# Four graph-attention layers on one core: broadcasting a row of factors by DMA and a ScalarE copy instead of TensorE transposes

## The chip, the cores and the metric

The kernel runs on one core of one Trainium2 chip. The metric is the time of one execution on the device in microseconds (us). TensorE (PE) multiplies matrices, VectorE (DVE), ScalarE (ACT) and GpSimd (POOL) work element by element, and SyncE (SP) here only issues DMA transfers. Each engine has its own queue of instructions, and semaphores make one engine wait for another.

## The reference, cut to what matters

The input x has 16 batch items of 1024 nodes with 256 features, in float32. Four layers follow each other, and each adds to x the output of a graph attention over one 1024 x 1024 adjacency matrix. Layers 0 and 2 have 4 heads of 64 features, layers 1 and 3 have one head of 256.

```python
h = jnp.maximum(_layernorm(x, axis=-1), 0.0)
# one layer, one head, with Wh = h @ W:
e = e_src[:, None] + e_dst[None, :]          # e_src = Wh @ a[:D], e_dst = Wh @ a[D:]
e = jnp.where(e > 0, e, slope * e)
e = jnp.where(adj, e, -inf)
h_prime = softmax(e, axis=-1) @ Wh
x = x + elu(h_prime)                         # relu in layer 3
```

The kernel uses that exp of a leaky relu of a sum is a maximum of two products. A factor that depends on the row i alone falls out of the softmax, so that the weight of node j for node i is mask(j, i) times max(g(i), r(j)), and the rest of the exponent, which depends on j alone, is multiplied into the rows of Wh. With j on the 128 partitions, r(j) is a scalar of the partition, but g(i) has to stand in every partition as a row of 1024 numbers. How this row comes to be in all partitions is what the change is about.

## The kernel before

A **step** is one layer of one batch item; there are 64 steps, 32 of a 4-head layer and 32 of a 1-head layer, and four batch items are interleaved. Every step is cut into eight **positions**, one for each group of its aggregation. Each engine's instructions run in the order of the program. The preparation of step n + 2 is spread over the positions from the start of step n on (in the steady part of the program) by this table, whose entries are positions after the plan was made:

```python
WBUFS = 21
PREPARATION = (0, 0, 1, 2, 3, 3, 4, 4, 5, 5, 5, 5, 6, 6, 7, 7, 8)
# pieces: stats(0), stats(1), normalise(0), normalise(1), transpose x2, project x4,
#         transpose x2, project x4, factors
```

So `factors` of a step falls on position 0 of the step ahead of it. The pieces that matter here:

```python
def normalise(half):                                    # ScalarE
    xn = st["xn", half] = prep.tile([P, HALF, F], F32, name="t4", bufs=3)
    for q in range(HALF):
        c = half * HALF + q
        nc.scalar.activation(xn[:, q, :], xs[b][:, c, :], AF.Identity,
                             bias=st["shift"][:, c:c + 1], scale=st["rstd"][:, c:c + 1])

def transpose(half, k):                                 # TensorE, then ScalarE to hT
    pt = ps_p.tile([P, HALF, P], F32, name="pp")        # ps_p has two buffers
    for q in range(HALF):
        nc.tensor.transpose(pt[:, q, :], st["xn", half][:, q, k * P:(k + 1) * P], ident)
    nc.scalar.activation(st["hT", half][:, k, :], pt.rearrange("p q i -> p (q i)"), AF.Relu)

def project(c):                                         # TensorE from hT; ScalarE empties pw
    pw = ps_p.tile([P, F + 2 * H], F32, name="pp")
    ...

def factors():
    ...                                                 # rcol, gcol: exp on ScalarE
    nc.gpsimd.tensor_scalar(gcol, gcol, EXP_SHIFT, None, op0=ALU.min)

def broadcast(n, h):                                    # g(i) into all partitions
    g = state[n]["g", h] = ps_g.tile([P, N], F32, name="g")
    for c in range(C):
        nc.tensor.transpose(g[:, c * P:(c + 1) * P],
                            state[n]["gcol"][:, c, h:h + 1].to_broadcast([P, P]), ident)

def weights(n, h, jc):                                  # VectorE, 128 x 1024
    w = state[n]["w", h, jc] = work.tile([P, N], F32, name="w", bufs=WBUFS)
    nc.vector.scalar_tensor_tensor(w, state[n]["g", h], state[n]["rcol"][:, jc, h:h + 1],
                                   mask[:, jc, :], op0=ALU.max, op1=ALU.mult)
```

`aggregate` multiplies eight such tiles `w` of a head with `whx` on TensorE into `acc` (two buffers) and copies `acc` to `y` on ScalarE. What ends a step, `finish`, is spread over positions 0 to 3 of the next step:

```python
def scaled(half):                                       # GpSimd: yh *= r; then
    e = st["e", half] = prep.tile([P, HALF * H, D], F32, name="t4", bufs=3)
    nc.gpsimd.tensor_scalar(e, yh, 0.0, -3.0e38, op0=ALU.min, op1=ALU.max)
def exponential(half):
    nc.scalar.activation(st["e", half], st["e", half], AF.Exp)
def add(half):                                          # not in the last layer
    nc.vector.scalar_tensor_tensor(e, e, -1.0, yh, op0=ALU.add, op1=ALU.max)
    nc.gpsimd.tensor_add(xh, xh, e)
return [(0, divide), (0, lambda: scaled(0)), (1, lambda: scaled(1)),
        (1, lambda: exponential(0)), (2, lambda: exponential(1)),
        (2, lambda: add(0)), (3, lambda: add(1))]
```

`xn` and `e` are both named `t4` and share one ring of three buffers. One position of the main loop is, in the order of the program:

```python
emit_tiles(place[n, h, C - 1] + 1, must=True)   # tiles w that this group needs
aggregate(n, h, i0, per)
while ending and ending[0][0] <= k:             # pieces of the last step's finish
    ending.pop(0)[1]()
prepare(8 * n + k)                              # pieces of preparation due here
emit_tiles(min(done["tiles"] + ahead, done["free"] + WBUFS))   # tiles w ahead of need
```

`emit_tiles` calls `broadcast` for a head when the next tile is within four of it, and only once the preparation of its step is complete.

Of the kernel before, what the change touches and what calls it, by code (L numbers as in the profile page):

```python
# [24 lines left out]
F32 = mybir.dt.float32  # L25
# [3 lines left out]
AF = mybir.ActivationFunctionType  # L29
# [4 lines left out]
P = 128  # L34
# [1 line left out]
SHIFT = 60.0  # L36
EXP_SHIFT = math.exp(SHIFT)
STREAMS = 4
WBUFS = 21
PREPARATION = (0, 0, 1, 2, 3, 3, 4, 4, 5, 5, 5, 5, 6, 6, 7, 7, 8)  # L40


LAYERS = [
# [8 lines left out]
def kernel(ctx: ExitStack, tc: tile.TileContext, x, adj, ws, avs, out):  # L52
    nc = tc.nc
    B, N, F = x.shape
    C = N // P
# [5 lines left out]
    ident = const.tile([P, P], F32, name="ident")  # L61
# [17 lines left out]
    with tc.tile_pool(name="wprep", bufs=2) as wp, tc.tile_pool(  # L79
        name="wpsum", bufs=2, space=PSUM  # L80
    ) as wps:
        for l, (H, slope, hs, _) in enumerate(LAYERS):
# [3 lines left out]
            for part in range(2):  # L86
                nc.scalar.dma_start(
                    out=a_bc[:, part],
                    in_=bass.AP(tensor=avs[l].tensor, offset=avs[l].offset + part * D,
                                ap=[[0, P], [hs, H], [1, D]]),  # L90
# [24 lines left out]
    with tc.tile_pool(name="mprep", bufs=2) as mp, tc.tile_pool(  # L115
        name="mpsum", bufs=2, space=PSUM
# [16 lines left out]
    small = ctx.enter_context(tc.tile_pool(name="small", bufs=4))  # L133
    work = ctx.enter_context(tc.tile_pool(name="work", bufs=2))
    ps_g = ctx.enter_context(tc.tile_pool(name="ps_g", bufs=2, space=PSUM))
    ps_acc = ctx.enter_context(tc.tile_pool(name="ps_acc", bufs=2, space=PSUM))
    ps_p = ctx.enter_context(tc.tile_pool(name="ps_p", bufs=2, space=PSUM))

    L = len(LAYERS)
# [2 lines left out]
    state = [dict() for _ in steps]  # L142
# [5 lines left out]
    def preparation(n):  # L148

        b, l = steps[n]  # L150
        H, slope, _, _ = LAYERS[l]
        D = F // H
        st = state[n]

        def stats(half):
            if half == 0:
                st["mv"] = small.tile([P, C, 2], F32, name="mv")
                st["bn"] = small.tile([P, C, 6], F32, name="bn")
            for c in range(half * HALF, (half + 1) * HALF):
                nc.vector.bn_stats(st["bn"][:, c, :], xs[b][:, c, :])  # L160
                nc.vector.bn_aggr(st["mv"][:, c, :], st["bn"][:, c, :])  # L161
            if half == 1:
                rstd = st["rstd"] = small.tile([P, C], F32, name="rstd")
                nc.gpsimd.tensor_scalar(rstd, st["mv"][:, :, 1], EPS, None, op0=ALU.add)
                nc.gpsimd.tensor_tensor(rstd, rstd, neghalf, op=ALU.pow)  # L165
                shift = st["shift"] = small.tile([P, C], F32, name="shift")
                nc.gpsimd.tensor_tensor(shift, st["mv"][:, :, 0], rstd, op=ALU.mult)
                nc.gpsimd.tensor_scalar(shift, shift, -1.0, None, op0=ALU.mult)

        def normalise(half):  # L170
# [6 lines that stand above are left out]
        def transpose(half, k):  # L177
            if k == 0:
                st["hT", half] = prep.tile([P, K, HALF * P], F32, name="hT")
            pt = ps_p.tile([P, HALF, P], F32, name="pp")  # L180
            for q in range(HALF):
                nc.tensor.transpose(pt[:, q, :], st["xn", half][:, q, k * P:(k + 1) * P], ident)  # L182
            nc.scalar.activation(st["hT", half][:, k, :], pt.rearrange("p q i -> p (q i)"),  # L183
                                 AF.Relu)

        def project(c):
            if c == 0:
                st["whx"] = prep.tile([P, C, H, D + 1], F32, name="whx", bufs=3)
                st["sd"] = small.tile([P, C, 2 * H], F32, name="sd")
            whx = st["whx"]  # L190
            half, q = divmod(c, HALF)
            pw = ps_p.tile([P, F + 2 * H], F32, name="pp")
            for k in range(K):
                nc.tensor.matmul(pw, lhsT=st["hT", half][:, k, q * P:(q + 1) * P],  # L194
                                 rhs=wx[l][:, k, :], start=(k == 0), stop=(k == K - 1))
            nc.scalar.activation(whx[:, c, :, D], pw[:, F + H:F + 2 * H], AF.Exp, bias=nbias[l],  # L196
                                 scale=slope)
            nc.scalar.activation(st["sd"][:, c, :], pw[:, F:F + 2 * H], AF.Copy)
            if H == 1:
                nc.scalar.activation(whx[:, c, 0, 0:D], pw[:, 0:D], AF.Copy,  # L200
                                     scale=whx[:, c, 0, D:D + 1])
            else:
                nc.scalar.activation(whx[:, c, :, 0:D],  # L203
                                     pw[:, 0:F].rearrange("p (h d) -> p h d", h=H), AF.Copy)
                nc.gpsimd.tensor_tensor(whx[:, c, :, 0:D], whx[:, c, :, 0:D],  # L205
                                        whx[:, c, :, D:D + 1].to_broadcast([P, H, D]),
                                        op=ALU.mult)

        def factors():
            sd = st["sd"]  # L210
            rcol = st["rcol"] = small.tile([P, C, H], F32, name="rcol")
            nc.scalar.activation(rcol, sd[:, :, H:2 * H], AF.Exp, bias=rbias[l],
                                 scale=1.0 - slope)
            gcol = st["gcol"] = small.tile([P, C, H], F32, name="gcol")
            nc.scalar.activation(gcol, sd[:, :, 0:H], AF.Exp, bias=rbias[l],
                                 scale=-(1.0 - slope))
            nc.gpsimd.tensor_scalar(gcol, gcol, EXP_SHIFT, None, op0=ALU.min)  # L217

        out = [lambda: stats(0), lambda: stats(1), lambda: normalise(0), lambda: normalise(1)]
        for half in range(2):  # L220
            out += [lambda half=half, k=k: transpose(half, k) for k in range(K)]
            out += [lambda c=c: project(c) for c in range(half * HALF, (half + 1) * HALF)]

        return list(zip(PREPARATION, out + [factors], strict=True))

    def broadcast(n, h):

        g = state[n]["g", h] = ps_g.tile([P, N], F32, name="g")
        for c in range(C):
            nc.tensor.transpose(g[:, c * P:(c + 1) * P],  # L230
                                state[n]["gcol"][:, c, h:h + 1].to_broadcast([P, P]), ident)

    def weights(n, h, jc):

        w = state[n]["w", h, jc] = work.tile([P, N], F32, name="w", bufs=WBUFS)
        nc.vector.scalar_tensor_tensor(w, state[n]["g", h], state[n]["rcol"][:, jc, h:h + 1],  # L236
# [72 lines left out]
    def groups(n):  # L309
        if LAYERS[steps[n][1]][0] == 1:  # L310
# [3 lines left out]
    tiles = [(n, h, jc) for n, (b, l) in enumerate(steps) for h in range(LAYERS[l][0])  # L314
             for jc in range(C)]
    place = {t: i for i, t in enumerate(tiles)}
    done = {"tiles": 0, "g": 0, "free": 0, "prepared": 0, "wanted": 0}
    agenda = []

    def prepare(upto):  # L320

        while agenda and (agenda[0][0] <= upto or agenda[0][1] < done["wanted"]):
            _, n, piece, last = agenda.pop(0)
            piece()
            if last:
                done["prepared"] = n + 1

    def plan(n, at):
        new = preparation(n)
        agenda.extend((at + k, n, piece, i == len(new) - 1) for i, (k, piece) in enumerate(new))  # L330
        agenda.sort(key=lambda a: a[:2])

    def emit_tiles(upto, must=False):
        while done["tiles"] < min(upto, len(tiles)):
            i = done["tiles"]

            while done["g"] <= min(i + C // 2, len(tiles) - 1):
                n, h, _ = tiles[done["g"]]
                if n >= done["prepared"]:
                    if i < done["g"] or not must:  # L340
                        break
                    done["wanted"] = n + 1
                    prepare(-1)
                broadcast(n, h)
                done["g"] += C
            if i >= done["g"]:
                return
            weights(*tiles[i])
            done["tiles"] += 1
# [8 lines left out]
    for n in range(2):  # L358
        plan(n, -99)
        prepare(0)  # L360
    ending = []
    with tc.manual_schedule():
        for n in range(len(steps)):
            for k, (h, i0, per) in enumerate(groups(n)):
# [10 lines left out]
                ahead = 4 if per > 1 else 2  # L375
                emit_tiles(min(done["tiles"] + ahead, done["free"] + WBUFS))
            for _, piece in ending:
# [42 lines left out]
```

## Time and profile before

| What | Value |
|---|---|
| Time, median of 3 runs | 2822.34 us (2819.63 to 2822.93) |
| Span of the profiled execution | 2823.2 us |
| DVE busy | 1986.5 us, 70% |
| ACT busy | 1054.9 us, 37% |
| POOL busy | 897.0 us, 32% |
| DMA, mean over the span | 16 GB/s |

Busy time is the sum of an engine's instructions; those of PE are pipelined, so that a busy PE is not PE at its peak. The chain of work that ended last is followed back from the last instruction, at each step to what released it or to the instruction before it on its engine. The list of waits gives for each pair of waiter and releaser the total in us, the number of times and the longest. In the timeline, a line gives the start, the duration, the engine, the line of the kernel, the operation, output and inputs, and in square brackets the idle time just before it and who ended it.

### The profile page before, as it was taken

How to read it: one execution, taken by the hardware profiler on the slowest of the kernel's cores; microseconds unless marked ns; L12 is line 12 of the kernel's file. 1: busy time of each engine (PE TensorE's matmuls, PEld its weight loads, DVE VectorE, ACT ScalarE, POOL GpSimd, SP SyncE). 2: the span in 40 equal slices, each digit the busy share in tenths (PEclk: the TensorE clock that was granted, in tenths of full speed). 3: DMA queues.
4: the chain of work that ended last, by engine and by line, in shares of the span. 5: the costliest groups of instructions: out<-in, count | busy, mean ns of one | idle time of the engine just before them, and what ended most of it. 6: DMA issues, size and time to landing. Idle time of an engine off the chain costs nothing.

```text
span 2823.2 us, 90054 instructions
## 1 busy us (share of the span) xinstructions
PE 2675.6 (95%) x41296; PEld 2387.0 (85%) x41296; DVE 1986.5 (70%) x2569; ACT 1054.9 (37%) x3041; POOL 897.0 (32%) x909
## 2 busy tenths in 40 slices
PE   1899999999999999999999999999999999999998
PEld 1788888888988888888988889888898888888887
DVE  6597675576975678748777469667696577875672
ACT  0423424343333343343344343343333334344331
POOL 0233424233223244243242243333423324324221
PEclk9999999999999999999999999999999999999999
DMA  4000000000000000000100000000010000000000
GB/s 143 7 3 2 2 2 2 2 32 9 25 32 15 18 2 3 2 1 32 32 2 32 31 2 3 2 2 17 16 33 17 16 32 2 3 2 1 17 17 30
DMA packets 38842, 45.60 MB, mean 16 GB/s; under 512 B 3136, under 2 KB 37440, under 8 KB 38464
## 3 DMA queue, kind: packets, MB, share of 16 engines
q1 hardware_dynamic: 35776, 38.80, 4.1%
q8 instruction: 324, 5.31, 0.8%
q10 hardware_dynamic: 2688, 1.05, 0.1%
q14 instruction: 54, 0.44, 0.1%
HBM read 23.07 MB, written 16.78 MB: 14 GB/s over the span
## 4 chain that ended last, share of the span: by engine, by line
PE 89%; DVE 5%; ACT 3%; DMA 1%; POOL 1%; issue 1%; DVEq 0%; ACTq 0%; SPq 0%; POOLq 0%
PE acc L252 64%; PE pp L194 16%; PE g L230 5%; PE pp L182 4%; DVE w L236 3%; ACT whx L196 1%; ACT whx L200 1%; DMA a_bc<-in_L_gnn_a 1%; ACT y L256 1%; DVE bn L160 0%; ACT whx L203 0%; DVE mask L129 0%; POOL gcol L217 0%; DVE t L292 0%; DVE mv L161 0%
## 5 line engine op out<-in xcount | busy, mean ns | idle before, releaser
L252 PE MATMUL acc<-whx,w 128*64 128x65 f32 x36864 | 1939.1, 241 | 21.7 <-DVE w L236 21.6
L252 PEld LDWEIGHTS acc<-whx,w 128*64 128x64 f32 x36864 | 1749.9, 145 | 180.0 <-issue 41.1
L236 DVE SCALAR_TENSOR_TENSOR w<-g,rcol,mask 128x1024 f32<-128x1024 f32 x1280 | 1544.1, 1273 | 419.7 <-PE acc L252 249.5
L256 ACT ACTIVATE y<-acc 128x260 f32<-128x260 f32 (+1 forms) x512 | 197.8, 386 | 1433.0 <-PE acc L252 1433.0
L194 PE MATMUL pp<-wx,hT 128*128 128x258 f32 (+1 forms) x2048 | 509.1, 392 | 2.0 <-ACT hT L183 2.0
L277 POOL TENSOR_TENSOR y<-y,r 128x1024 f32<-128x1024 f32 x128 | 242.8, 1898 | 814.3 <-DVE r L273 814.3
L194 PEld LDWEIGHTS pp<-wx,hT 128*128 128x128 f32 x2048 | 379.4, 190 | 67.1 <-ACT hT L183 3.0
L205 POOL TENSOR_TENSOR whx<-whx 128x256 f32<-128x256 f32 x256 | 157.7, 617 | 599.0 <-ACT whx L203 599.0
L293 POOL TENSOR_TENSOR x<-x,t 128x1024 f32<-128x1024 f32 x96 | 227.2, 2366 | 227.2 <-DVE t L292 227.2
L174 ACT ACTIVATE t<-x,shift,rstd 128x256 f32<-128x256 f32 x512 | 265.2, 590 | 47.7 <-POOL x L293 42.5
L273 DVE RECIPROCAL r<-y 128x32 f32<-128x32 f32 (+1 forms) x64 | 17.7, 277 | 324.5 <-ACT y L256 324.5
L196 ACT ACTIVATE whx<-pp,nbias 128x4 f32<-128x4 f32 (+1 forms) x512 | 135.3, 264 | 192.0 <-PE pp L194 179.1
L230 PE MATMUL g<-ident,gcol 128*128 128x128 f32 x1280 | 169.6, 275 | 38.8 <-POOL gcol L217 38.8
L160 DVE BATCH_NORM_STATS2 bn<-x 128x6 f32<-128x256 f32 x512 | 200.7, 392 | 2.2 <-DMA x<-in_x 2.2
L230 PEld LDWEIGHTS g<-ident,gcol 128*128 128x128 f32 x1280 | 142.1, 137 | 59.4 <-POOL gcol L217 50.9
L182 PE MATMUL pp<-ident,t 128*128 128x128 f32 x1024 | 153.0, 282 | 27.8 <-ACT t L174 12.7
L182 PEld LDWEIGHTS pp<-ident,t 128*128 128x128 f32 x1024 | 110.9, 141 | 70.5 <-ACT whx L200 28.0
L183 ACT ACTIVATE hT<-pp 128x512 f32<-128x512 f32 x256 | 145.9, 595 | 20.7 <-PE pp L182 19.1
L292 DVE SCALAR_TENSOR_TENSOR t<-t,y 128x1024 f32<-128x1024 f32 x96 | 118.6, 1235 | 39.4 <-ACT t L286 39.4
L200 ACT ACTIVATE whx<-pp,whx 128x256 f32<-128x256 f32 x256 | 121.4, 474 | 0.0
L165 POOL TENSOR_TENSOR rstd<-rstd,neghalf 128x8 f32<-128x8 f32 x64 | 106.7, 1666 | 5.3
L161 DVE BATCH_NORM_AGGREGATE mv<-bn 128x2 f32<-128x6 f32 x512 | 92.8, 181 | 16.9
(35 smaller groups left out, 593.7 us busy)
## 6 DMA issues: line engine op xcount, KB each, us to landing
x<-in_x SPq DMA_DIRECT2D x16, 1024.0 KB, 5.3
out<-x SPq DMA_DIRECT2D x32, 512.0 KB, 3.1
a_raw<-in_adj SPq DMA_DIRECT2D x8, 512.0 KB, 3.7
a_bc<-in_L_gnn_a ACTq DMA_DIRECT2D x8, 128.0 KB, 5.9
wx<-in_L_gnn_W SPq DMA_DIRECT2D x4, 256.0 KB, 12.4
```

The costliest lines, as they stand in the source:

```text
L160: nc.vector.bn_stats(st["bn"][:, c, :], xs[b][:, c, :])
L174: nc.scalar.activation(xn[:, q, :], xs[b][:, c, :], AF.Identity, bias=st["shift"][:, c:c + 1], scale=st["rstd"][:, c:c + 1])
L182: nc.tensor.transpose(pt[:, q, :], st["xn", half][:, q, k * P:(k + 1) * P], ident)
L194: nc.tensor.matmul(pw, lhsT=st["hT", half][:, k, q * P:(q + 1) * P], rhs=wx[l][:, k, :], start=(k == 0), stop=(k == K - 1))
L196: nc.scalar.activation(whx[:, c, :, D], pw[:, F + H:F + 2 * H], AF.Exp, bias=nbias[l], scale=slope)
L205: nc.gpsimd.tensor_tensor(whx[:, c, :, 0:D], whx[:, c, :, 0:D], whx[:, c, :, D:D + 1].to_broadcast([P, H, D]), op=ALU.mult)
L230: nc.tensor.transpose(g[:, c * P:(c + 1) * P], state[n]["gcol"][:, c, h:h + 1].to_broadcast([P, P]), ident)
L236: nc.vector.scalar_tensor_tensor(w, state[n]["g", h], state[n]["rcol"][:, jc, h:h + 1], masks[LAYERS[steps[n][1]][3]][:, jc, :], op0=ALU.m ...
L252: nc.tensor.matmul(acc[o % P:o % P + cols, q, :], lhsT=st["w", h, jc][:, o:o + cols], rhs=st["whx"][:, jc, h, :], start=(jc == 0), stop=(j ...
L256: nc.scalar.activation(st["y"][:, i0:i0 + per, h, :], acc, AF.Copy)
L277: nc.gpsimd.tensor_tensor(yh, yh, r[:, :, None].to_broadcast([P, HALF * H, D]), op=ALU.mult)
L293: nc.gpsimd.tensor_add(xh, xh, e)
```

## The change: a row in DRAM, a broadcasting DMA and a copy

The change takes the broadcast off TensorE. A new piece `rows`, one position after `factors`, transposes all of a step's `gcol` at once on TensorE, copies the result to SBUF on ScalarE and stores it as rows of 1024 numbers in DRAM. A DMA then reads one row into all 128 partitions (`fetch`), and ScalarE copies it from there into the PSUM tile `g` that VectorE reads as before. Rows are fetched up to two heads ahead of the head that was broadcast last. Two more buffers of 128 x 1024 for the fetched rows take their room from the tiles `w`, of which 19 are left. The rows of x are normalised by ScalarE in both kernels, in `normalise`, which the change leaves as it is.

```diff
-WBUFS = 21
-PREPARATION = (0, 0, 1, 2, 3, 3, 4, 4, 5, 5, 5, 5, 6, 6, 7, 7, 8)
+WBUFS = 19
+PREPARATION = (0, 0, 1, 2, 3, 3, 4, 4, 5, 5, 5, 5, 6, 6, 7, 7, 8, 9)
...
+    dram = ctx.enter_context(tc.tile_pool(name="dram", bufs=4, space=bass.MemoryType.DRAM))
...
+        def rows():
+            pt = ps_p.tile([C * H, P], F32, name="pp")
+            nc.tensor.transpose(pt, st["gcol"].rearrange("p c h -> p (c h)"), ident)
+            gT = small.tile([C * H, P], F32, name="gT", bufs=2)
+            nc.scalar.activation(gT, pt, AF.Copy)
+            st["grow"] = dram.tile([H, C, P], F32, name="grow")
+            nc.sync.dma_start(out=st["grow"].rearrange("h c i -> c h i"), in_=gT)
...
-        return list(zip(PREPARATION, out + [factors], strict=True))
+        return list(zip(PREPARATION, out + [factors, rows], strict=True))
+
+    def fetch(n, h):
+        gs = state[n]["gs", h] = work.tile([P, N], F32, name="gs", bufs=2)
+        nc.sync.dma_start(out=gs, in_=state[n]["grow"][h].rearrange("c i -> (c i)")
+                          .partition_broadcast(P))
 
     def broadcast(n, h):
         g = state[n]["g", h] = ps_g.tile([P, N], F32, name="g")
-        for c in range(C):
-            nc.tensor.transpose(g[:, c * P:(c + 1) * P],
-                                state[n]["gcol"][:, c, h:h + 1].to_broadcast([P, P]), ident)
+        nc.scalar.activation(g, state[n]["gs", h], AF.Copy)
...
+    def fetch_heads():      # called when a step is prepared, and after each broadcast
+        while done["gs"] < min(done["g"] + 2 * C, len(tiles)):
+            n, h, _ = tiles[done["gs"]]
+            if n >= done["prepared"]:
+                break
+            fetch(n, h)
+            done["gs"] += C
```

More of the change, by code (lines that the diff above doesn't have):

```diff
@@ L316 @@
     place = {t: i for i, t in enumerate(tiles)}
-    done = {"tiles": 0, "g": 0, "free": 0, "prepared": 0, "wanted": 0}
+    done = {"tiles": 0, "g": 0, "gs": 0, "free": 0, "prepared": 0, "wanted": 0}
     agenda = []
@@ L326, in prepare @@
                 done["prepared"] = n + 1
+                fetch_heads()
     def plan(n, at):
@@ L345, in emit_tiles @@
                 done["g"] += C
+                fetch_heads()
             if i >= done["g"]:
```

## The prediction, made before the changed kernel was run

> **What bounds the kernel now.** I read the page first: busy times, then the chain of work that ended last. TensorE is busy nearly all the time, and the chain lies on it for 89%. The transposes that broadcast g (line 230) are 5% of the span there, about 141 us.
>
> ```profile
> PE 2675.6 (95%) x41296; PEld 2387.0 (85%) x41296; DVE 1986.5 (70%) x2569; ACT 1054.9 (37%) x3041; POOL 897.0 (32%) x909
> ...
> PE 89%; DVE 5%; ACT 3%; DMA 1%; POOL 1%; issue 1%; DVEq 0%; ACTq 0%; SPq 0%; POOLq 0%
> PE acc L252 64%; PE pp L194 16%; PE g L230 5%; PE pp L182 4%; DVE w L236 3%; ACT whx L196 1%; ACT whx L200 1%; DMA a_bc<-in_L_gnn_a 1%; ACT y L256 1%; DVE bn L160 0%; ACT whx L203 0%; DVE mask L129 0%; POOL gcol L217 0%; DVE t L292 0%; DVE mv L161 0%
> ```
>
> What the removed work takes from the end time I read from the chain in order of time (start, us, what) between 1000 and 1100 us: a broadcast of eight transposes advances TensorE by 0.87 to 1.02 us.
>
> ```profile
> 1019.18 0.87 PE g L230 x8
> ...
> 1032.93 1.02 PE g L230 x8
> ```
>
> The list of TensorE's waits adds one that goes with it: it stands 38.8 us waiting for gcol where the broadcast directly follows `factors`.
>
> ```profile
> PE g L230 <- POOL gcol L217: 38.8, 32, 1.3
> ...
> PE acc L252 <- DVE w L236: 21.6, 28, 0.9
> ```
>
> 23 of the 28 waits for a weight tile fall before 420 us, by the same list cut to windows, where VectorE is behind. Later TensorE waits for hardly anything: after 1000 us it never waited for a weight tile.
>
> Last, the timeline of one 1-head step, whose first aggregation starts at S = 2460.35 us. It decides my prediction.
>
> ```profile
> 2465.26 1.09 PE L230 MATMUL g<-ident,gcol 128*128 128x128 f32 x8 [1.26 <-POOL gcol L217]
> ...
> 2466.46 4.86 DVE L236 SCALAR_TENSOR_TENSOR w<-g,rcol,mask 128x1024 f32<-128x1024 f32 x4 [2.90 <-PE g L230]
> ...
> 2471.23 1.22 DVE L292 SCALAR_TENSOR_TENSOR t<-t,y 128x1024 f32<-128x1024 f32 x1
> ...
> 2472.54 2.36 POOL L293 TENSOR_TENSOR x<-x,t 128x1024 f32<-128x1024 f32 x1 [1.65 <-DVE t L292]
> ...
> 2474.94 2.08 ACT L174 ACTIVATE t<-x,shift,rstd 128x256 f32<-128x256 f32 x4 [0.26 <-POOL x L293]
> ...
> 2478.14 1.09 ACT L183 ACTIVATE hT<-pp 128x512 f32<-128x512 f32 x2
> ...
> 2481.86 1.90 PE L194 MATMUL pp<-wx,hT 128*128 128x258 f32 x8
> ```
>
> See a chain that is not on the page's: the weight tiles wait for g; `add(0)` stands behind them in VectorE's queue; GpSimd's sum follows; the second `normalise` waits for that sum (its 0.26 us), because its tile takes the t4 buffer of e(0), three allocations earlier; `hT` stands behind it in ScalarE's queue; and the projection needs `hT`. hT ends at 2479.23, the projection starts at 2481.86: **2.6 us of slack**.
>
> **What the Trainium skill says.** "DMA: Bandwidth & Descriptors", section "Anatomy of one DMA — SWDGE (gpsimd) path", fits a DMA (on another issue path than here) as about 2.0 us fixed plus bytes over 436 GB/s, so 512 KB take 3.2 us. The trace agrees: the 512 KB issues below land after 3.1 and 3.7 us. It has no small one, so 2.0 us for the new store is an estimate from that page.
>
> ```profile
> out<-x SPq DMA_DIRECT2D x32, 512.0 KB, 3.1
> a_raw<-in_adj SPq DMA_DIRECT2D x8, 512.0 KB, 3.7
> ```
>
> "DMA: Bandwidth & Descriptors", section "Two DMAs through the same engine are not ordered", says that a DMA reading what another wrote must await its semaphore: store and fetch add up. "TensorE: Matmul & The Clock Gate", section "Architectural detail: the array is 16× 32×32, not 1× 128×128", says ScalarE and VectorE are strict FIFO: a ScalarE copy that waits for a DMA holds everything behind it. The trace shows such order: hT runs only after the waiting normalise. "ScalarE: Activation LUTs", section "What ACT_TABLE_LOAD costs", gives 186 ns + 0.833 ns an element without pointer operands: 1039 ns for 1024. The trace has 1048 ns for the exp of 128x1024 (line 286).
>
> **The change, part by part.**
>
> *Removed from TensorE*: 160 broadcasts x 0.95 us (middle of 0.87 and 1.02) = 152 us, and the 38.8 us of waiting for gcol, since `rows` comes a position later: 191 us. Before 280 us VectorE is the bound, and 13 of the broadcasts are there: take off 12 us. *Added to TensorE*: 64 small transposes at 0.16 us (the chain has four of line 182 in 0.65): 10 us. **Net gain 169 us.**
>
> *Added to ScalarE*: 160 copies x 1.05 us = 168 us; with the small ones some 1,240 us, 45%. No bound. *Added to DMA*: 160 x 512 KB = 84 MB; at 1.2 us each (3.2 less 2.0) 190 us, beside other work.
>
> *Moved*: the time at which g is ready. I wrote out the order of pieces by position from the code. In 26 steady 1-head steps the first broadcast of the next step stands in position 1, right behind `rows`, so ScalarE waits there for store and fetch. Their delay D, from the copied row to the fetched one, is 2.0 (store) + 3.6 (fetch, from 3.1 to 3.7) + 0.4 (an issue takes 0.37 us on SP) = 6.0 us.
>
> From S, with the durations of the trace: two aggregations of 3.48 and the small transpose 7.2; y 0.39, exp 1.05, row copied (0.2) 8.8; D 14.8; copy to PSUM 15.85; two weight tiles 2.47, 18.3; add(0) 1.22, 19.5; GpSimd's sum 2.36, 21.9; normalise 2.08, 24.0; y and hT 1.4, **25.4**. TensorE, with no broadcast in the way, has four aggregations, the small transpose, 0.9 of transposes and a fifth aggregation behind it at 4 x 3.48 + 0.2 + 0.9 + 3.48 = **18.5** and then waits for hT: **6.9 us**. (The slack of 2.6 is spent: the chain moves back by 6.5, TensorE forward by 3.) In three of the 26 the step before is a last layer, which has no e, so the ring does not tie; 23 x 6.9 = **159 us lost**.
>
> *Six boundaries, four early and two at the end,* where the plan was made at position 4: the rows come at position 5 of the step ahead. From there the first eight tiles need 7.5 us (D, the copies) + 8 x 1.21 = 17 us, and TensorE has two positions left. At the last two these are about 8 and 7 us of work: 9 + 10 us lost. At the four early ones projections fill the positions, and VectorE has other tiles to make meanwhile; I choose 5 us each. Sum 39 us.
>
> *Two 4-head steps in a row* occur six times. From 2371.5 to 2416.4 VectorE has no gap: its 45 us are just TensorE's 45. With four broadcasts (3.8 us) fewer, TensorE outruns it, and of that about 2.7 us come back as waits: 16 us. For ScalarE being in the way of `pp` (14.6 us of such waits now) I add 8 us by choice.
>
> Sum: -169 + 159 + 39 + 16 + 8 = +53, so **2875 us**, 1.9% above 2822.
>
> **Rivals.** (1) *TensorE gets the whole gain*: 2822 - 169 = 2653. For it: 89% of the chain is TensorE, ScalarE is at 37%, and two `acc` buffers let TensorE run past a short ScalarE stall. Against it: the slack of 2.6 us, and that the wait comes in front of hT. (2) *The same chain with a slower DMA*: every us of D costs 23 us and about 6 more at the six boundaries; D of 8 gives 2933. For it: 128 readers of the same 4 KB, and two fetches issued together. Against: 16 DMA engines that are nearly idle. A D of 4.5 gives 2832. (3) *VectorE becomes the bound*: 1986 of some 2650 is 75%, so only in the pairs and at the start; two w buffers fewer shorten its lead by 2.5 us. This alone gives 2653 + 16 and, by choice, some 20 for the lead: 2690.
>
> **Range and chances.** D between 4.5 and 8 gives 2832 to 2933. Wider below, since a part of the chain that I have put in series may overlap: 2790. Above, since another engine's wait may add to it: 2950. The point lies just below the 2% line (2879), so same and slower share most of the chance; faster by over 2% needs the chain to be mostly hidden.
>
> **What would show it.** In the changed profile: line 230 off TensorE; new waits of TensorE for hT (line 183, as waits of the projections), some 23 of about 7 us; ScalarE waiting about 4 us for the DMA of gs in 1-head steps; normalise waiting for GpSimd's sum far longer than 42.5 us in total; store and fetch landing in about 2.0 and 3.6 us. I am wrong if TensorE's waits stay near 100 us in total: then ScalarE was not held, or the ring does not tie; or if the fetch lands much later.

## The result: 2755.6 us, and the profile after

| | Kernel before | Changed kernel |
|---|---|---|
| Time, median | 2822.64 us (4 runs) | 2755.64 us (4 runs) |
| Ratio to before, 95% interval | 1 | 0.977 (0.974 to 0.979) |
| TensorE (PE) busy | 2675.6 us | 2581.3 us |
| ScalarE (ACT) busy | 1054.9 us | 1199.6 us |
| mean granted TensorE clock | 0.994 | 0.987 |

The last three rows are of the profiled executions.

The change makes the kernel 2.3% faster. The prediction was 2875 us with a range of 2790 to 2950 us: wrong in direction, and the time lies 34 us below the range.

The page of the changed kernel, busy times and the chain of work that ended last:

```profile
PE 2581.3 (94%) x40080; PEld 2268.5 (82%) x40080; DVE 1984.5 (72%) x2569; ACT 1199.6 (44%) x3265; POOL 896.6 (33%) x909
...
PE 72%; DVE 14%; DMA 6%; ACT 4%; issue 3%; POOL 1%; DVEq 0%; ACTq 0%; SPq 0%; POOLq 0%
PE acc L266 53%; PE pp L195 15%; DVE w L250 11%; DMA gs<-grow 4%; PE pp L183 3%; DMA grow<-gT 2%; DVE bn L161 1%; ACT t L300 1%; ACT g L245 1%; DVE t L306 1%; DVE mv L162 1%; ACT whx L197 1%; DMA a_bc<-in_L_gnn_a 1%; ACT whx L201 0%; ACT y L270 0%
```

The broadcast is gone from TensorE's part of the chain. In its place the chain now passes through the weight tiles of VectorE (11%, from 3%) and through the new DMAs (4% and 2%): TensorE is still the engine that is nearly always busy, but it has lost some of its distance from the others.

TensorE's waits in the changed kernel (waiter, releaser, total us, times, longest):

```profile
PE acc L266 <- DVE w L250: 56.9, 84, 1.2
...
PE acc L266 <- ACT y L270: 18.1, 19, 1.6
...
PE pp L223 <- POOL gcol L218: 3.0, 2, 1.8
PE pp L195 <- ACT hT L184: 2.7, 3, 1.8
```

The wait for gcol is down from 38.8 to 3.0 us, as predicted. The wait for hT, which the prediction put at some 159 us, is 2.7 us. A wait for y of 18.1 us is new, and the wait for tiles w grew from 21.6 to 56.9 us.

The timeline of one 1-head step; its first aggregation starts at 2389.57 us:

```profile
2397.96 0.25 ACT L225 ACTIVATE gT<-pp 32x128 f32<-32x128 f32 x1
...
2404.29 1.03 ACT L245 ACTIVATE g<-gs 128x1024 f32<-128x1024 f32 x1 [4.11 <-DMA gs<-grow]
...
2405.67 3.75 PE L266 MATMUL acc<-whx,w 128*128 128x257 f32 x16 [1.03 <-ACT y L270]
2406.46 2.06 ACT L175 ACTIVATE t<-x,shift,rstd 128x256 f32<-128x256 f32 x4
2407.74 1.22 DVE L306 SCALAR_TENSOR_TENSOR t<-t,y 128x1024 f32<-128x1024 f32 x1
...
2408.70 1.06 ACT L184 ACTIVATE hT<-pp 128x512 f32<-128x512 f32 x2
...
2409.05 2.37 POOL L307 TENSOR_TENSOR x<-x,t 128x1024 f32<-128x1024 f32 x1 [8.92 <-DVE t L306]
2409.33 2.06 PE L195 MATMUL pp<-wx,hT 128*128 128x258 f32 x8
```

Two things are to be seen. ScalarE stands for 4.11 us in front of the copy of g, as reckoned: from the end of gT (2398.21) to the start of the copy are 6.1 us. But the second `normalise` (line 175) starts at 2406.46, before `add(0)` (line 306, 2407.74) and GpSimd's sum (line 307, 2409.05), for which it waited in the kernel before. It isn't tied to them, so hT is there in time, and TensorE loses only the 1.03 us of its wait for y.

The chain in order of time gives the two parts of the delay, store and fetch (start, us, what):

```profile
2398.24 1.78 DMA grow<-gT
...
2400.09 4.12 DMA gs<-grow
```

### The profile page after: what moved, and what is told of

It reads as the page before. It is cut to its first block, busy times and chain, and to the rows that moved or that the text cites. A ratio compares the mean times of both kernels' runs of the same rounds, so it can differ in the third digit from the quotient of the medians.

```text
span 2756.5 us, 88771 instructions
## 1 busy us (share of the span) xinstructions
PE 2581.3 (94%) x40080; PEld 2268.5 (82%) x40080; DVE 1984.5 (72%) x2569; ACT 1199.6 (44%) x3265; POOL 896.6 (33%) x909
## 4 chain that ended last, share of the span: by engine, by line
PE 72%; DVE 14%; DMA 6%; ACT 4%; issue 3%; POOL 1%; DVEq 0%; ACTq 0%; SPq 0%; POOLq 0%
PE acc L266 53%; PE pp L195 15%; DVE w L250 11%; DMA gs<-grow 4%; PE pp L183 3%; DMA grow<-gT 2%; DVE bn L161 1%; ACT t L300 1%; ACT g L245 1%; DVE t L306 1%; DVE mv L162 1%; ACT whx L197 1%; DMA a_bc<-in_L_gnn_a 1%; ACT whx L201 0%; ACT y L270 0%
## 5 line engine op out<-in xcount | busy, mean ns | idle before, releaser
L266 PE MATMUL acc<-whx,w 128*64 128x65 f32 x36864 | 1965.4, 242 | 77.9 <-DVE w L250 56.9
L250 DVE SCALAR_TENSOR_TENSOR w<-g,rcol,mask 128x1024 f32<-128x1024 f32 x1280 | 1543.3, 1273 | 523.4 <-ACT g L245 432.7
L195 PE MATMUL pp<-wx,hT 128*128 128x258 f32 (+1 forms) x2048 | 515.8, 395 | 2.9 <-ACT hT L184 2.7
L175 ACT ACTIVATE t<-x,shift,rstd 128x256 f32<-128x256 f32 x512 | 264.8, 588 | 78.7 <-POOL x L307 56.6
L245 ACT ACTIVATE g<-gs 128x1024 f32<-128x1024 f32 x160 | 163.5, 1022 | 129.5 <-DMA gs<-grow 128.0
L183 PE MATMUL pp<-ident,t 128*128 128x128 f32 x1024 | 155.4, 284 | 34.0 <-ACT t L175 18.9
L306 DVE SCALAR_TENSOR_TENSOR t<-t,y 128x1024 f32<-128x1024 f32 x96 | 118.4, 1233 | 35.4 <-ACT t L300 35.3
L296 POOL TENSOR_SCALAR t<-y 128x1024 f32<-128x1024 f32 x96 | 101.7, 1060 | 8.5
## 6 DMA issues: line engine op xcount, KB each, us to landing
a_bc<-in_L_gnn_a ACTq DMA_DIRECT2D x8, 128.0 KB
```

Of the source, the lines that this page charges most:

```text
L245: nc.scalar.activation(g, state[n]["gs", h], AF.Copy)
L266: nc.tensor.matmul(acc[o % P:o % P + cols, q, :], lhsT=st["w", h, jc][:, o:o + cols], rhs=st["whx"][:, jc, h, :], start=(jc == 0), stop=(j ...
```

## The experiments

Ten kernels ran; each time is a median of four runs or more, and each ratio is to the kernel before, run beside it on the same chip, where it took 2823.6 to 2824.2 us. Differences to the changed kernel are taken from its 2755.6 us above, beside which the kernel before took 2822.6 us; its four runs lie between 2751.2 and 2761.0 us, so a difference of a few us to it says little.

### Where the predicted wait went: the buffer put back

In the built programs each tile has an address. In the kernel before the second `xn` of a 1-head step has that of e(0) in 25 steps. In the changed kernel it has, in exactly 23 of these steps, the address of the first `xn` of the same step, which comes free when TensorE has transposed it. The three t4 buffers are not handed out in turn. The waits of `normalise` for GpSimd's sum say the same, first in the kernel before, then in the changed one:

```profile
ACT t L174 <- POOL x L293: 42.5, 38, 2.6
...
ACT t L175 <- POOL x L307: 56.6, 15, 5.0
```

Before, 23 of the 38 waits last about 0.26 us, as in the prediction's step, and 15, which lie in 4-head steps, 2.3 to 2.6 us. After the change the 23 are gone and the 15 last 2.9 to 5.0 us. The experiment puts the old choice back, in these 1-head steps alone:

```diff
-            xn = st["xn", half] = prep.tile([P, HALF, F], F32, name="t4", bufs=3)
+            held = state[n - 3].get(("e", 0)) if half == 1 and n >= 3 else None
+            if held is not None and LAYERS[steps[n - 2][1]][0] == 1 and ready_at[n] < n - 3:
+                xn = st["xn", half] = held.rearrange("p (c h) d -> p c (h d)",
+                                                     h=LAYERS[steps[n - 3][1]][0])
+            else:
+                xn = st["xn", half] = prep.tile([P, HALF, F], F32, name="t4", bufs=3)
```

> The changed kernel with one thing put back: in the 23 steady 1-head steps the second normalise again writes into the buffer of e(0) of the step before, as it does in the kernel before; in the changed kernel it got the buffer of the first normalise instead. Nothing else differs, in order or in buffers. Theory A (the prediction's chain is right, and only the buffer it runs through was wrong): TensorE waits some 6 us more in each of the 23 steps, 23 x (6.9 - 1.0) = 136 us, so 2870 to 2905 us, with TensorE waiting for hT about 23 times. Theory B (ScalarE and TensorE have more slack than I reckoned, so that the wait does not reach TensorE whatever the buffer): within 10 us of the changed kernel, 2745 to 2766 us.

Measured: 2920.2 us, ratio 1.034 (1.032 to 1.036): 164.5 us slower than the changed kernel, and slower than the kernel before. Theory B is out: the wait is there as soon as the buffer is e(0)'s. Its waits for GpSimd's sum, and its list of TensorE's waits:

```profile
ACT t L180 <- POOL x L312: 168.4, 38, 5.0
...
PE pp L200 <- ACT hT L189: 115.4, 26, 4.9
PE acc L271 <- DVE w L255: 53.0, 77, 0.9
```

Of the 38 waits, 15 are those of the changed kernel, and the other 23 now last 4.86 us each. A few other tiles of the ring get other buffers with this edit too, but none of TensorE's other waits grew.

And the timeline of one of its 1-head steps, to be held against the one above:

```profile
2548.77 1.03 ACT L250 ACTIVATE g<-gs 128x1024 f32<-128x1024 f32 x1 [3.82 <-DMA gs<-grow]
...
2552.22 1.22 DVE L311 SCALAR_TENSOR_TENSOR t<-t,y 128x1024 f32<-128x1024 f32 x1
...
2553.52 2.35 POOL L312 TENSOR_TENSOR x<-x,t 128x1024 f32<-128x1024 f32 x1 [8.63 <-DVE t L311]
...
2555.90 2.07 ACT L180 ACTIVATE t<-x,shift,rstd 128x256 f32<-128x256 f32 x4 [4.86 <-POOL x L312]
...
2558.15 1.06 ACT L189 ACTIVATE hT<-pp 128x512 f32<-128x512 f32 x2
2558.78 3.42 PE L200 MATMUL pp<-wx,hT 128*128 128x258 f32 x8 [4.88 <-ACT hT L189]
```

This is the prediction's chain, link by link: copy, add(0), sum, normalise (4.86 us behind the sum), hT, and TensorE waiting 4.88 us. With the 0.74 us of its wait for y in the same step TensorE loses 5.6 us, where the prediction said 6.9.

The time rose by 164.5 us, beyond the 136 expected. The waits for hT account for 115.4 - 2.7 = 113 us, and TensorE's busy time rose by 2636.4 - 2581.3 = 55 us; together 168. With it the granted clock fell from 0.987 to 0.964: the projection behind the wait takes 3.42 us, in place of 2.06 in the changed kernel's step above. The same step in windows, PEclk the third figure from the end:

```profile
2553.00:2558.00 5.00, 0.89 (x5) 0.43 (x3) 5.00 (x5) 2.10 (x5) 3.31 (x2) 1.00 0.01 2
2558.00:2562.00 4.00, 3.22 (x8) 2.64 (x9) 4.00 (x5) 3.20 (x8) 1.39 (x1) 0.57 0.19 72
2562.00:2570.00 8.00, 7.79 (x39) 6.37 (x39) 3.30 (x3) 3.78 (x12) 0.00 (x0) 1.00 0.11 31
```

After the wait the granted clock is 0.57 for some 4 us. The Trainium skill, "TensorE: Matmul & The Clock Gate", section "Part 1: The HAM clock gate (the "warmup" mystery)", says that TensorE goes to half its clock after about 3.4 us of idleness; this trace agrees, with one wait of 4.88 us. It does not take so long a wait, though: in the kernel with the later copy (below), waits of 1.87 and 0.86 us, the second up to 1383.48 us, were followed by a clock of 0.51 from 1384.65 to 1388.10 us.

### What the removed broadcasts cost

```diff
-        for c in range(C):
+        for c in (*range(C), *range(C)):
```

> The kernel before with each of the 160 broadcasts done twice over (the same eight transposes into the same tile again): the cost of the removed work by itself. By the prediction's 0.95 us each: 152 us more, less some 12 us at the start where VectorE is the bound: 2950 to 2975 us. If the transposes are partly hidden (behind waits of TensorE, or because their weights load beside other work): under 2920 us.

Measured: 2958.0 us, ratio 1.047 (1.046 to 1.049): 133.8 us for 160 broadcasts, 0.84 us each. The expected 140 us (152 less 12) were 6 too many; the cost of the removed work was sized well.

### Is a tile w worth something? 18 and 19 tiles

The first attempt frees the second `normalise` in all steps, with a fourth t4 buffer, and pays with one tile w:

```diff
-WBUFS = 19
+WBUFS = 18
-            xn = st["xn", half] = prep.tile([P, HALF, F], F32, name="t4", bufs=3)
+            xn = st["xn", half] = prep.tile([P, HALF, F], F32, name="t4", bufs=4)
```

(and the same for `e`).

> The changed kernel with four buffers for t4 in place of three, so that the second normalise waits for no other tile in any step; one tile w fewer (18) makes the room. Theory A: the 56.6 us in which ScalarE waits for the sum on GpSimd go, but hardly any of it reached TensorE, so 2740 to 2756 us. Theory C (the lead of VectorE, that is the number of w buffers, is what the changed kernel now lives on): slower by 10 us or more, 2766 us and up.

Measured: 2773.6 us, ratio 0.982 (0.981 to 0.984), 18 us slower than the changed kernel: theory C. To tell the tile from the buffers, the tile alone:

```diff
-WBUFS = 19
+WBUFS = 18
```

> The changed kernel with 18 tiles w in place of 19 and nothing else: what one tile of VectorE's lead is worth. Theory C (the run with four t4 buffers lost 18 us by its one tile w fewer, and not by its buffers): 2768 to 2778 us. Theory A' (the loss there came from the freed buffers, which change the order in which things are done): 2751 to 2761 us, as the changed kernel.

Measured: 2775.3 us, ratio 0.983 (0.981 to 0.984). So one tile w costs 19.6 us, and a fourth t4 buffer is worth nothing beside it: in the run with four, all of ScalarE's 56.6 us of waits for the sum are gone from the list, and the time is still that of 18 tiles. TensorE's wait for tiles w, 56.9 us with 19 tiles, is with 18:

```profile
PE acc L266 <- DVE w L250: 72.0, 102, 1.4
```

The same question in the kernel before, with the two tiles taken that the change took:

```diff
-WBUFS = 21
+WBUFS = 19
```

> The kernel before with 19 tiles w in place of 21: the price of the room that the change took for fetched rows, by itself. In the kernel before TensorE waits for tiles w for 21.6 us only, nearly all before 420 us, so theory A: within 6 us of 2822 us. Theory C in its strong form (every tile is worth some 15 us in this kernel too): 2845 us and up.

Measured: 2827.5 us, ratio 1.002 (1.001 to 1.002): 3.9 us for two tiles. With the broadcasts on TensorE the lead hardly counts; without them the 19th tile is worth 19.6 us. The change has made VectorE a near second bound.

### Earlier and later rows

First, the copy of g two positions later in the steady part, so that ScalarE does not stand in front of it:

```diff
+                if not must and done["now"] < done["when"].get(n, 0):
+                    break
                 if n >= done["prepared"]:
...
                 done["prepared"] = n + 1
+                if done["now"] % 8 == 1:
+                    done["when"][n] = done["now"] + 2
...
+                done["now"] = 8 * n + k
```

> The changed kernel with the first copy of g of a step emitted two positions after the rows, and not right behind them, in the steady part: ScalarE then no longer stands waiting for the fetch in 1-head steps. Theory A: the 18 us of TensorE waiting for y go and little else changes: 2735 to 2750 us. Theory C (tiles come later to VectorE, and its lead is what counts): no gain or slower, 2756 us and up.

Measured: 2837.8 us, ratio 1.005 (1.003 to 1.007), 82 us slower than the changed kernel: theory C. TensorE's waits for y are gone from its list, but those for tiles w are 136.2 us. VectorE in a 1-head step:

```profile
2489.84 9.63 DVE L250 SCALAR_TENSOR_TENSOR w<-g,rcol,mask 128x1024 f32<-128x1024 f32 x8 [3.21 <-ACT g L245]
2500.46 2.48 DVE L250 SCALAR_TENSOR_TENSOR w<-g,rcol,mask 128x1024 f32<-128x1024 f32 x2 [0.99 <-ACT g L245]
2508.03 0.20 DVE L287 RECIPROCAL r<-y 128x8 f32<-128x8 f32 x1 [5.09 <-ACT y L270]
```

It makes ten tiles and then stands for 5.09 us, since the program hands out two tiles a position and the first two positions are lost. In this program the second `xn` also has e(0)'s buffer again, in 25 steps, so that it is not a change of one thing; with no tiles in front of `add(0)` that tie shows no new wait of TensorE for hT (2.7 us, as in the changed kernel).

Second, the rows one position earlier:

```diff
-PREPARATION = (0, 0, 1, 2, 3, 3, 4, 4, 5, 5, 5, 5, 6, 6, 7, 7, 8, 9)
+PREPARATION = (0, 0, 1, 2, 3, 3, 4, 4, 5, 5, 5, 5, 6, 6, 7, 7, 8, 8)
```

> The changed kernel with the rows in the same position as the factors, one position earlier. The fetch then lands some 3.5 to 5.5 us sooner, at the price of TensorE waiting for gcol again. Prediction's terms: 38.8 us come back as that wait (and 28 more steps than before might have it, as all 64 steps now do the transpose right behind the factors: up to 64 x 1.3 = 80 us); against it the 18 us of waits for y and most of the waits for w at the six boundaries (20 to 30 us) go. Sum: 2745 to 2795 us, 2765 us the middle. If it comes out under 2745 us, the time at which g arrives counted for more than I reckon.

Measured: 2798.7 us, ratio 0.991 (0.990 to 0.993), 43 us slower than the changed kernel and just above the expected span. Its waits:

```profile
PE pp L223 <- POOL gcol L218: 79.6, 64, 1.8
PE acc L266 <- DVE w L250: 31.6, 44, 1.9
```

All 64 transposes now wait for gcol (79.6 us, the upper figure expected), and only 25 us of waits for w go. The waits for y, which were expected to go, stay at 15.0 us. The extra position of the rows pays for itself.

### Without the copy to PSUM

```diff
-        g = state[n]["g", h] = ps_g.tile([P, N], F32, name="g")
-        nc.scalar.activation(g, state[n]["gs", h], AF.Copy)
+        state[n]["g", h] = state[n]["gs", h]
```

(and rows fetched one head ahead instead of two).

> The changed kernel without the copy to PSUM: VectorE reads the fetched row where the DMA put it. 160 copies (163.5 us of ScalarE) go, ScalarE never waits for a fetch, and g is ready 1 us sooner. Theory A: the 18 us of TensorE waiting for y go, and a few us at the boundaries, if a weight tile takes VectorE the same 1273 ns from SBUF as from PSUM: 2725 to 2750 us. Theory C: if a tile takes longer from SBUF (or GpSimd and VectorE get in each other's way there), VectorE, which is without slack in two 4-head steps in a row, makes it slower than the changed kernel: every 10 ns a tile are 13 us of VectorE.

Measured: 2913.4 us, ratio 1.032 (1.030 to 1.034): 158 us slower than the changed kernel. The groups by form (busy us, mean ns, then idle time before):

```profile
L248 DVE SCALAR_TENSOR_TENSOR w<-gs,rcol,mask 128x1024 f32<-128x1024 f32 x1280 | 1852.6, 1514 | 424.0 <-DMA gs<-grow 250.1 <-PE pp L182 147.0 <-ACT y L268 15.7
...
L205 POOL TENSOR_TENSOR whx<-whx 128x256 f32<-128x256 f32 x256 | 332.9, 1316 | 254.7 <-ACT whx L203 254.1
L305 POOL TENSOR_TENSOR x<-x,t 128x1024 f32<-128x1024 f32 x96 | 313.4, 3264 | 384.8 <-DVE t L304 382.5 <-PE acc L264 2.3
```

A tile takes 1514 ns on average in place of 1273, which are 309 us more of VectorE, and GpSimd's instructions are longer too: 1316 ns from 618 and 3264 from 2362. TensorE's waits for w rise from 56.9 to 164.4 us. That the rows are fetched one head ahead does not explain it: VectorE's idle time in front of the tiles fell, from 523.4 us to 424.0.

The average of 1514 ns hides two kinds of tiles. In the trace, the 614 tiles with no GpSimd instruction beside them took 1274 ns on average and 1289 at most, as with g in PSUM; the 666 that met one took 1735 ns on average and up to 3390. GpSimd's product of 128x256 took 622 ns on average where it met no tile, and 1901 where it did. In the changed kernel the longest of all tiles took 1285 ns. So SBUF as the source is not slow by itself; the meeting with GpSimd is what costs. The Trainium skill, "SBUF — State Buffer", section "SBUF: two separate sides", says that VectorE with two SBUF inputs and GpSimd exclude each other on a shared pair of ports for a whole instruction; this trace agrees, in that both get longer and only where they meet. The copy on ScalarE is not a detour: it keeps this input out of SBUF.

### A faster version

If a tile w is worth 18 us and a fetch takes 4 us while the heads follow each other at some 10, one buffer for the fetched row should do, and its room can hold a tile:

```diff
-WBUFS = 19
+WBUFS = 20
-        gs = state[n]["gs", h] = work.tile([P, N], F32, name="gs", bufs=2)
+        gs = state[n]["gs", h] = work.tile([P, N], F32, name="gs", bufs=1)
-        while done["gs"] < min(done["g"] + 2 * C, len(tiles)):
+        while done["gs"] < min(done["g"] + C, len(tiles)):
```

> The changed kernel with one buffer for the fetched row in place of two, each row fetched one head ahead, and the room given to a 20th tile w. If a tile of VectorE's lead is worth some 18 us here too (as from 18 to 19), and one buffer for the row is enough because a fetch takes about 4 us and the heads of a step follow each other at some 10 us: 2730 to 2745 us. If the gain per tile ends at 19, or the single row buffer holds ScalarE in front of the second head: 2750 us and up.

Measured: 2738.3 us, ratio 0.969 (0.968 to 0.971), 17 us below the changed kernel. TensorE's list puts half of what its waits lost on w (56.9 to 48.5 us) and half on y (18.1 to 9.7 us), so that the gain is not the tile's alone: fetching one head ahead came with it, and the two were not run apart. On top of it, earlier rows only at the six boundaries:

```diff
-        return list(zip(PREPARATION, out + [factors, rows], strict=True))
+        at = PREPARATION if ready_at[n] < n - 3 else PREPARATION[:-1] + (8,)
+        return list(zip(at, out + [factors, rows], strict=True))
```

> The same, and in the steps whose preparation was planned at position 4 (the prediction's six boundaries, four early and two late) the rows come one position earlier, with the factors. The prediction put 39 us on these boundaries for coming a position later; one position is 3.5 to 6 us of that at each, less 1.3 us of TensorE waiting for gcol: 12 to 25 us less than without it. If the boundaries cost little, no difference.

Measured: 2725.7 us, ratio 0.965 (0.964 to 0.967), 12.5 us less again, and the fastest of all: 3.5% below the kernel before. Its waits for w are down, from 48.5 us, to:

```profile
PE acc L267 <- DVE w L251: 38.7, 55, 1.5
```

Those for gcol are up from 2.9 to 10.0 us. In the profiled executions TensorE's idle time is the same in both versions (159 us), and the gain is in its busy time, which fell from 2578.3 to 2564.1 us with a granted clock of 0.991 in place of 0.986. Which waits had brought the clock down was not tested.

## Why the prediction was wrong

**The step that failed** is in the sentence "its tile takes the t4 buffer of e(0), three allocations earlier". I read from the kernel before that the second `normalise` waits for GpSimd's sum, explained it by a ring handed out in turn, and carried that over to the changed kernel. The explanation was right for these steps of the kernel before and not a rule: in the changed kernel the second `xn` was given another buffer, in 23 steps, as many as I had counted. The term built on it, 159 us, was in the run 18.1 us of waits for y and 2.7 us for hT; put back by the experiment, it was 164.5 us. The prediction named this case ("or the ring does not tie") as what would make it wrong, but gave it far too little chance. Why the builder chose so was not tested; the choice itself is seen in the addresses and in the 23 waits that are gone. It is not the copy on ScalarE that brings it about: in the kernel without the copy (line 174 there) `normalise` waits 23 times, 71.2 us in all, for the transposes that free the first `xn`.

The rest of the chain was right, but that 164.5 us comes so near to 159 is in part luck. TensorE's waits were shorter than reckoned (115.4 us for hT and 16.5 for y, together 132), and the 55 us of longer busy time that came with the lower clock, of which the prediction did not know, made up for it. With the tie in place the kernel took 2920 us, 45 more than the 2875 predicted.

**The other steps**, by their own numbers:

- *What is taken off TensorE*: 140 us for the broadcasts, 133.8 measured by doubling. The wait for gcol: 38.8 predicted, 35.8 gone. Right.
- *D, store and fetch*: 6.0 us predicted, 6.1 measured. The parts were 1.78 and 4.12 us in one step, with little between. ScalarE's wait in front of the copy was predicted at about 4 us and is 128.0 us in 34 times, 3.8 us each. Right.
- *ScalarE no bound*: about 1,240 us predicted, 1199.6 measured. Right.
- *The six boundaries*: 39 us predicted for all six. One position of it, taken back, is worth 12.5 us (in the version with 20 tiles). The whole was not measured by itself.
- *VectorE's lead*: rival 3 gave 2.5 us for the shorter lead of the changed kernel, and 20 by choice, and neither went into the sum. This was too small: the 19th tile is worth 19.6 us once TensorE is relieved, and TensorE's waits for w rose by 35 us.
- *The clock*: not in the prediction at all. The granted clock fell from 0.994 to 0.987.

How the gain of 67 us comes about: TensorE's busy time fell by 94.3 us and its idle time rose by 2756.5 - 2581.3 - (2823.2 - 2675.6) = 27.6 us. The idle time is nearly all in the waits listed: +35.3 for w, +18.1 for y, -35.8 for gcol, +6.2 for `normalise` (12.7 to 18.9), and small ones. The busy time fell by less than the 134 us, as the matmuls that stayed took longer (line 252, now 266: 1939.1 to 1965.4 us) and 64 small transposes came in. The lower clock fits the longer matmuls; how the 40 us divide between it and the transposes was not measured.

Had the wait been sized by the measured 21 us, the same sum would have been 2822 - 169 + 21 + 39 + 16 + 8 = 2737 us, 19 us below the measured time. The lead and the clock are what the sum leaves out; how the 19 us divide, and whether the 39, 16 and 8 are right, was not measured.

## What to carry to other kernels

A wait seen on a shared buffer belongs to one built program: after any change of order, look up which tile follows which in that buffer before you carry the wait over. When work is taken off the busiest engine, look at once for the engine that feeds it, since the depth of the buffers between them, worth next to nothing before (2 us a tile), can become the most valuable room there is (some 18 us a tile). And a copy that moves one of VectorE's two SBUF inputs into PSUM can pay for itself where GpSimd works at the same time.

## What the runs showed of the hardware

- A wait of TensorE of 4.88 us costs more than itself: the granted clock was 0.57 over the next 4 us, and eight matmuls of the projection took 3.42 us, in place of 2.06 and 1.90 in the steps shown of the other two kernels. In another kernel two waits of 1.87 and 0.86 us, close together, were followed by a clock of 0.51 for 3.4 us.
- VectorE's 128x1024 operation on two tensors took 1273 ns with one of them in PSUM. With both in SBUF it took 1274 ns where no GpSimd instruction ran beside it, and 1735 ns on average, up to 3390, where one did; GpSimd's product of 128x256 took 622 ns without such a tile beside it and 1901 ns on average with one.
- Fetching one row of 4 KB into all 128 partitions took 4.12 us where it was on the chain, and storing 16 KB took 1.78 us before it.
- A ScalarE copy of 128x1024 from SBUF to PSUM took 1022 ns.
